# Loading the sort's keys through GpSimd's DMA queue and the small identity table through SyncE's

## The chip, the cores and the metric

The kernel runs on one core of a Trainium2 chip. The metric is the device time of one execution in microseconds (us); a smaller number is better. A core has five engines that each work through their own list of instructions in order: TensorE (PE, matrix products and transposes), VectorE (DVE), ScalarE (ACT), GpSimd (POOL) and SyncE (SP). A transfer between device memory (HBM) and on-chip memory (SBUF) is issued by one of SP, ACT and POOL; in the profile SP and ACT feed the two "hardware dynamic" queues and POOL the one "software dynamic" queue. All three queues share the core's 16 DMA engines.

## What is computed

Sixteen graphs of 1024 nodes with 64 features go through four graph layers, each followed by a residual sum and a layer norm:

```python
# layer 0: x + leaky_relu((I - sqrt(d) A / sqrt(d)) @ (batchnorm(x) @ W0 + b0)), d = row sums of A
# layer 1: attention with 8 heads, logits g0 * q.k / 8 + g1 * adj
# layer 2: per node and feature, three quantiles over the (thinned) neighbours:
vals = jnp.where(nd[..., None], x[:, None, :, :], jnp.inf)
s = jnp.sort(vals, axis=2)                 # 1024 x 1024 x 64 values per graph
agg = sum(w * interpolate(s, tau) for tau, w in ((.25, .25), (.5, .5), (.75, .25)))
#          then two dense layers with a relu
# layer 3: adj @ (x @ W3) + b3
```

The quantiles of layer 2 are by far the largest part. The kernel does not sort per node: it sorts each feature's 1024 values once per graph, ranks them, and finds the wanted rank among a node's neighbours by bit counts that TensorE sums.

## The kernel before, in words

Graphs are handled in pairs, as 128 partitions (2 graphs x 64 features) for the sort and the quantiles. The outer loop (L1193) runs p from 0 to 8 and is a software pipeline over the eight pairs. One turn p holds:

- layers 0 and 1 of pair p (`layer0` for each of the two graphs, then `attention`), for p below 8
- the sort of pair p-1 (`sort_keys`, then `sort` inside `middle`), for p from 1 on
- layers 2 and 3 of pair p-2 (`ends`, `layers23`), for p from 2 on; the last pair's come after the loop
- the quantiles of pair p-1 (`quantiles`, L782), for p from 1 on; this is the long part, about 1.05 ms of each turn

So the same passage comes up again and again: a turn's quantiles end, and the next turn starts with `sort_keys`, layer 0 of a new pair and the last layers of an old one. It comes up for p = 2 to 7 in full. At p = 1 attention, not quantiles, stands ahead of it. At p = 8 there is no layer 0.

What the passage does around the change, by name and line:

- `sort_keys` (L1155) allocates the tile `key` (128x1024 float32, 512 KB) and loads it from the scratch tensor `x2T_d` in HBM. `x2T_d` was written by POOL at the end of the pair's attention (L645).
- The eight row blocks of graph 0's adjacency matrix go to the tiles `adj0` to `adj7` (L424, SP, 512 KB each), and ACT sums their rows (L425).
- `place_tables` (L309) loads `place` (128x1024 bf16, 256 KB) and `identb` (a 128x128 bf16 identity, 32 KB); DVE makes `negidb` and `noteye` from `identb` (L315, L317).
- `layer0` (L402) loads `x0` in two halves (L407, SP), normalises it on DVE (L410, L411), transposes it on PE (L289), multiplies by the weights (L305), scales by the degrees (L415, L427, L428), and then multiplies by the transposed adjacency matrix (L392), whose row blocks `at` come through SP (L330) into four buffers. From the same `at` blocks DVE makes the neighbour masks `nbt` (L333, L334).
- `sort` (L1096) is a bitonic network of 55 steps on DVE. A step is three operations (L1105): `mask` compares, two more write the new `key`. Each mask is stored to HBM through SP (L1131) and the mask tile has four buffers.
- `layers23` (L1017) loads `x2b`, `oT`, `tof`, `agg2` (1.5 MB through ACT, L1026) and its own `at` blocks (L1056, SP).
- The quantiles end with DVE's L919 (`res`), the product of a PSUM accumulator with weights, and its store to `agg_d` by POOL (L920). There are twelve such stores per turn.

Instructions are placed on each engine's list at build time by a scheduler with a cost model, so an edit of one line can move neighbours on other engines. Two kinds of waits are then added. The first is for data and for memory: `key`, for instance, takes the place in SBUF of tiles that the quantiles still use. The second belongs to the transfers themselves: the hardware queues share eight semaphores in turn, so that a transfer waits for the landing of the one that had its semaphore before. An SP instruction that waits holds up everything that stands behind it on SP's list.

Of the kernel before, what the change touches and what calls it, by code (L numbers as in the profile page):

```python
# [25 lines left out]
P = 128  # L26
# [84 lines left out]
def gnn_kernel(ctx: ExitStack, tc: tile.TileContext, a: dict, out: bass.AP):  # L111
    nc = tc.nc
# [90 lines left out]
    x2T_d = dram.tile([B // 2 * P, N], F32, name="x2T_d")  # L203
# [105 lines left out]
    def place_tables(l0):  # L309
        place = l0.tile([P, 8 * P], BF, name="place")  # L310
        nc.sync.dma_start(place, a["c_place"])
        identb = l0.tile([P, P], BF, name="identb")
        nc.scalar.dma_start(identb, a["c_idb"])
        negidb = l0.tile([P, P], BF, name="negidb")
        nc.vector.tensor_scalar(negidb, identb, -1.0, None, op0=ALU.mult)  # L315
        noteye = l0.tile([P, P], BF, name="noteye")
        nc.vector.tensor_scalar(noteye, negidb, 1.0, None, op0=ALU.add)  # L317
        return place, identb, negidb, noteye
# [835 lines left out]

    def sort_keys(srt, ip):  # L1155
        key = srt.tile([P, N], F32, name="key", bufs=2)
        nc.sync.dma_start(key, x2T_d[ds(ip * P, P)])
        return key

    def middle(keys, srt, key, pace=()):  # L1160
# [32 lines left out]
    for p in range(B // 2 + 1):  # L1193
        with double_banks(), ExitStack() as es:
            if p >= 1:
                keys = es.enter_context(tc.tile_pool(name="keys", bufs=1, reuse_waits="tile", side="right"))
                key = sort_keys(keys, p - 1)
            last = ends(p - 2) if p >= 2 else iter(())
            if p < B // 2:
                nat = es.enter_context(tc.tile_pool(name="nat", bufs=1, reuse_waits="tile"))  # L1200
                x2 = nat.tile([P, NB, 2, C], F32, name="x2")
                graphs = [Graph(bb=bb, x1=nat.tile(NODES, F32, name=f"x1_{bb}")) for bb in range(2)]
                adj = [nat.tile([P, N], F32, name=f"adj{k}") for k in range(NB)]
                wqkv = twice(nat, "wqkv", a["WqkvT"], 3 * H * C)
                with tc.tile_pool(name="l0", bufs=1, reuse_waits="tile") as l0:
                    tables = place_tables(l0)
                    for gr in graphs:
                        gr.adj = list(adj)
                        layer0(l0, tables, p, gr.bb, None if gr.bb else adj, gr.x1)
                        if gr.bb == 0:  # L1210
                            for part in (keys_of, gates, queries_of):
                                part(gr, nat, lambda i: None)
                            for k in range(NB):
                                gated(gr, k)
                            for _ in last:
                                pass
# [43 lines left out]
```

## Time and profile before

| | |
|---|---|
| three timed runs | 13429.87, 13438.83, 13460.58 us; median 13438.83 |
| the profiled execution | 13430.77 us, of which the core's span is 13428.9 us |
| busy in the span | PE 12106.3 us (90%), DVE 10731.4 (80%), ACT 7230.1 (54%), POOL 635.6 (5%) |
| mean granted TensorE clock | 0.948 |
| moved | HBM read 380.32 MB, written 116.59 MB; 37 GB/s over the span |
| `key` loads | 8, of 512 KB, issued by SP at 623.4, 2196.5, 3838.2, 5483.5, 7132.2, 8780.7, 10425.9 and 12071.2 us |
| `identb` loads | 8, of 32 KB, issued by ACT, one per turn p = 0 to 7 |

All times below are microseconds from the start of the span. In a timeline a row gives the start, the duration, the engine (SPq and ACTq are issues of transfers), the line, the operation, what it writes and reads, and in brackets how long the engine was idle before and what ended that. In the table of stretches a row gives the stretch, its length, the busy time of PE, PE's weight loads, DVE, ACT and POOL with the number of instructions, the granted clock, the mean busy share of the 16 DMA engines and GB/s. The chain of waits is the chain of work that ended last, followed back from the end.

### The profile page before, as it was taken

The numbers are of one execution on the slowest core, as the hardware profiler recorded it, in microseconds if no ns is written. First come the engines' busy times: TensorE is split into PE (matmuls) and PEld (weight loads), VectorE is DVE, ScalarE is ACT, GpSimd is POOL, SyncE is SP. The second block draws the span as 40 slices with busy tenths as digits, with TensorE's granted clock in tenths as the row PEclk, the third lists the DMA queues.
The fourth block names the chain that finished last, engine by engine and source line by source line (L and its number), as shares of the span: only waits on it lengthen the run. The fifth ranks groups of instructions, "written<-read, shape, count | busy, mean of one in ns | idle before, by whom it ended". The sixth has DMA issues, their size and how long they took to land.

```text
span 13428.9 us, 216352 instructions
## 1 busy us (share of the span) xinstructions
PE 12106.3 (90%) x85632; PEld 5237.5 (39%) x85632; DVE 10731.4 (80%) x18699; ACT 7230.1 (54%) x13164; POOL 635.6 (5%) x948
## 2 busy tenths in 40 slices
PE   7898997989979899798997989979899799993998
PEld 4554332543325433253333633335333353331332
DVE  3587887778877788777886788877888778978895
ACT  5665554655536555365553655546455465551553
POOL 0000000000000000000000010000100001000000
PEclk9999998999989999899998999989999899996998
DMA  2110003100031000310004100041000310002001
GB/s 78 69 63 19 5 5 105 57 17 5 5 121 42 15 6 5 131 34 14 5 5 132 32 14 5 5 134 38 6 5 20 121 36 7 8 22 77 4 5 44
DMA packets 356375, 510.90 MB, mean 38 GB/s; under 512 B 124448, under 2 KB 279584, under 8 KB 353312
## 3 DMA queue, kind: packets, MB, share of 16 engines
q1 hardware_dynamic: 288656, 371.94, 8.6%
q10 hardware_dynamic: 34192, 87.14, 1.9%
q0 software_dynamic: 32512, 38.00, 1.1%
q8 instruction: 673, 11.03, 0.3%
q14 instruction: 342, 2.80, 0.1%
HBM read 380.32 MB, written 116.59 MB: 37 GB/s over the span
## 4 chain that ended last, share of the span: by engine, by line
PE 66%; DVE 14%; issue 8%; DMA 3%; ACT 3%; POOL 0%; SPq 0%; DVEq 0%; ACTq 0%; POOLq 0%
PE bank L838 31%; PE acc L838 8%; PE banks L509 6%; PE bank L545 6%; PE bank L531 6%; PE wps L838 3%; DVE m L870 2%; DMA at<-in_adjT 2%; DVE key L1105 2%; PE bank L392 1%; PE bank L488 1%; PE banks L369 1%; PE bank L847 1%; DVE lt L853 1%; DVE mask L1105 1%
## 5 line engine op out<-in xcount | busy, mean ns | idle before, releaser
L870 DVE TENSOR_TENSOR m<-V,oh 128x3072 bf16<-128x3072 bf16 x1536 | 2640.2, 1753 | 312.9 <-PE wps L838 289.3
L838 PE MATMUL bank<-ndT,E 128*128 128x512 fp8e4 x11904 | 2751.7, 381 | 7.3
L900 ACT ACTIVATE vals<-bank 128x512 f32<-128x512 f32 x3072 | 1591.8, 602 | 1399.0 <-PE bank L838 1397.0
L516 DVE CUSTOM_DVE_ANT_0 s<-banks,adj 128x1024 f32<-128x1024 f32 x1024 | 1214.5, 1222 | 801.4 <-PE banks L509 798.4
L848 ACT ACTIVATE V<-bank 128x512 uint16<-128x512 f32 x1536 | 911.8, 597 | 1742.1 <-PE bank L838 1642.4
L838 PEld LDWEIGHTS <-E 128*128 128x128 bf16 x11904 | 1117.9, 98 | 1788.6 <-issue 551.0
L862 ACT CAST oh<-bank 128x512 f16<-128x512 f32 x3072 | 1577.6, 601 | 297.5 <-PE bank L838 297.3
L838 PE MATMUL bank<-oh,bd 128*128 128x512 f16 x6144 | 1480.0, 384 | 0.0
L535 ACT COPY pT<-bank 128x512 f32<-128x512 f32 x1536 | 800.6, 594 | 800.0 <-PE bank L531 799.9
L524 ACT ACTIVATE s<-s,mx 128x1024 f32<-128x1024 f32 x1024 | 1176.8, 1161 | 90.1 <-DVE mx L516 89.2
L509 PE MATMUL banks<-kT,qT 64*128 64x512 f32 x4096 | 1094.5, 625 | 65.7 <-DVE mx L516 36.1
L853 DVE TENSOR_TENSOR lt<-V,lim 128x2048 bf16<-128x2048 uint16 x768 | 935.1, 1218 | 221.5 <-PE bank L838 220.3
L531 PEld LDWEIGHTS bank<-ident,s 128*128 128x128 f32 x8192 | 883.9, 141 | 409.9 <-issue 285.7
L531 PE MATMUL bank<-ident,s 128*128 128x128 f32 x8192 | 1017.0, 277 | 9.3 <-ACT s L524 8.7
L545 PE MATMUL bank<-pT,v 128*64 128x256 f32 x8192 | 991.7, 385 | 0.0
L838 PEld LDWEIGHTS <-bd 128*128 128x128 f16 x6144 | 542.6, 98 | 889.4 <-issue 354.2
L838 PE MATMUL bank<-lt,dif 128*128 128x512 bf16 x3072 | 813.2, 381 | 51.9 <-DVE lt L853 30.9
L838 PE MATMUL acc<-vals,bonesf 128*32 128x512 f32 x6144 | 847.6, 603 | 0.0
L838 PE MATMUL wps<-m,tonesb 128*32 128x512 bf16 x9216 | 641.6, 382 | 78.7 <-DVE m L870 78.7
L838 PE MATMUL bank<-r,pen 32*128 32x512 f16 x6144 | 487.7, 384 | 241.0 <-DVE r L757 226.9
L545 PEld LDWEIGHTS bank<-pT,v 128*64 128x64 f32 x8192 | 544.7, 136 | 306.9 <-ACT pT L535 41.3
L838 PE MATMUL acc<-oh,base 128*32 128x512 f16 x9216 | 641.8, 384 | 0.0
(248 smaller groups left out, 13323.0 us busy)
## 6 DMA issues: line engine op xcount, KB each, us to landing
at<-in_adjT SPq DMA_DIRECT2D x256, 512.0 KB, 5.5
masks_d<-mask SPq DMA_DIRECT2D x440, 128.0 KB, 1.7
mask<-masks_d SPq DMA_DIRECT2D x440, 128.0 KB, 2.1
adj<-in_adj SPq DMA_DIRECT2D x96, 512.0 KB, 5.3
ad<-in_adj ACTq DMA_DIRECT2D x64, 512.0 KB, 6.4
agg_d<-vals POOLq DMA_DIRECT2D x96, 256.0 KB, 2.3
agg<-agg_d ACTq DMA_DIRECT2D x16, 1536.0 KB, 8.0
nd_d<-nd SPq DMA_DIRECT2D x128, 128.0 KB, 1.9
```

The costliest lines, as they stand in the source:

```text
L509: then(nc.tensor.matmul(ss[h][:, hf * 512:(hf + 1) * 512], gr.qk[hp, 0][HALF[h], k * P:(k + 1) * P], gr.qk[hp, 1][HALF[h], hf * 512:(hf + ...
L516: last = nc.vector.tensor_tensor_reduce(s, ss[h], gr.adj[k], -1.0, 3.0e38, ALU.add, ALU.min, mx)
L524: then_act(nc.scalar.activation(s, s, AF.Exp, bias=mx, scale=-1.0, accum_out=sm))
L531: then(nc.tensor.transpose(ps[:, m, :], exps[h][0][:, (4 * mh + m) * P:(4 * mh + m + 1) * P], ident))
L535: then_act(nc.scalar.copy(dst, ps))
L545: then(nc.tensor.matmul(po[HALF[h]], gr.v[:, 4 * mh + m, (2 * hp + h) * C:(2 * hp + h + 1) * C], pT[h][mh][:, m, :], start=(mh == 0 and m ...
L838: then(nc.tensor.matmul(*args, **kw))
L848: nc.scalar.activation(gr.V[g][:, w, cols], ps, AF.Copy, bias=OFF)
L853: nc.vector.tensor_tensor(u.lt, gr.V[g][:, None, 0, :].to_broadcast([P, 2, N]), gr.lim[q], ALU.is_lt)
L862: nc.scalar.copy(oh[:, kk, cols], ps)
L870: nc.vector.tensor_tensor(u.m[kk], gr.V[g].bitcast(BF), u.oh[s][:, kk, None, :].to_broadcast([P, NW, N]), ALU.mult)
L900: nc.scalar.activation(vals[t], ys[t], AF.Relu)
```

## The change

Two lines change. The load of `key` moves from SP's queue to POOL's, and the load of `identb` from ACT's queue to SP's, right behind `place`. Sizes, tiles, sources and everything else stay.

```diff
     def place_tables(l0):
         place = l0.tile([P, 8 * P], BF, name="place")
         nc.sync.dma_start(place, a["c_place"])
         identb = l0.tile([P, P], BF, name="identb")
-        nc.scalar.dma_start(identb, a["c_idb"])
+        nc.sync.dma_start(identb, a["c_idb"])
...
     def sort_keys(srt, ip):
         key = srt.tile([P, N], F32, name="key", bufs=2)
-        nc.sync.dma_start(key, x2T_d[ds(ip * P, P)])
+        nc.gpsimd.dma_start(key, x2T_d[ds(ip * P, P)])
         return key
```

In the program as built the lists change near the passages only. On POOL the key's load stands directly behind the turn's last `agg_d` store (L920), or at p = 1 behind the store of `x2T_d`. On SP, `place`, `identb`, the two halves of `x0` and the first four `at` blocks stand directly behind the eight `adj` loads, and two instead of one of `layers23`'s `at` blocks come ahead of the second four of layer 0. On DVE the first four entries of a passage are the same as before (`negidb`, `noteye`, the first `mask`, one half of the new `key`); then L410 of layer 0 comes two entries earlier (and L411 two), and some operations of the following 40 us change places (L372 ahead of L437, the second graph's L410 and L411 earlier, the first graph's L455 and L460 later). About 80 us after the end of the quantiles the lists agree again.

## Prediction

> **What bounds the kernel now.** I read the page first (busy time by engine, then the chain that ended last), then the passages where the moved loads stand, by stretches of 10 us and by the timelines of SP, DVE and POOL, and asked which wait ends last there. One warning: the chain puts 2199.41 to 2208.13 down to the `agg_d` store, but DVE's wait just there is for `x0`; I go by the timeline.
>
> ```profile
> span 13428.9 us, 216352 instructions
> PE 12106.3 (90%) x85632; PEld 5237.5 (39%) x85632; DVE 10731.4 (80%) x18699; ACT 7230.1 (54%) x13164; POOL 635.6 (5%) x948
> ...
> PE 66%; DVE 14%; issue 8%; DMA 3%; ACT 3%; POOL 0%; SPq 0%; DVEq 0%; ACTq 0%; POOLq 0%
> ```
>
> TensorE carries the chain, and DMA holds only 3% of it, some 400 us over nine passages. The change touches nothing in the quantiles or attention, so it can only move the passages. The passage of p = 2 in stretches of 10 us:
>
> ```profile
> 2160.00:2170.00 10.00, 10.00 (x75) 3.06 (x71) 0.05 (x1) 4.45 (x8) 0.54 (x1) 0.73 0.92 342
> 2170.00:2180.00 10.00, 10.00 (x88) 3.26 (x82) 0.00 (x0) 4.13 (x8) 0.00 (x0) 1.00 0.26 106
> ...
> 2200.00:2210.00 10.00, 0.53 (x3) 0.53 (x4) 5.37 (x11) 0.68 (x2) 0.00 (x0) 0.64 1.05 380
> ...
> 2220.00:2230.00 10.00, 6.63 (x49) 1.95 (x47) 3.13 (x8) 1.68 (x4) 0.00 (x0) 0.67 0.94 363
> ```
>
> The DMA engines are full while the `adj` blocks come (2160 to 2170), idle from about 2173 to 2196 under PE's last quantile products, and full again from 2198 to 2240, when PE and DVE starve. SP's timeline gives the reason:
>
> ```profile
> 2159.52 4.48 SPq L424 DMA_DIRECT2D adj<-in_adj  x8
> 2196.45 0.33 SPq L1157 DMA_DIRECT2D key<-x2T_d  x1
> 2196.88 0.38 SPq L311 DMA_DIRECT2D place<-in_c_place  x1
> ...
> 2198.33 3.42 SPq L330 DMA_DIRECT2D at<-in_adjT  x4
> ```
>
> SP stands 32 us at `key`. In the program as built that load waits for the quantiles' last product with `oh` and `bd`, whose SBUF it takes over; that product ends at 2196.42. DVE in the same place:
>
> ```profile
> 2198.42 0.69 DVE L919 TENSOR_TENSOR vals<-acc,cf 128x512 f32<-128x512 f32 x1 [38.37 <-PE acc L838]
> ...
> 2207.52 0.69 DVE L410 TENSOR_TENSOR y<-x,bn_a 128x512 f32<-128x512 f32 x1 [4.31 <-DMA x<-in_x]
> ...
> 2225.45 0.70 DVE L333 TENSOR_SCALAR nbt<-at 128x1024 bf16<-128x1024 f32 x1 [3.15 <-DMA at<-in_adjT]
> ```
>
> From L919 to 2250, DVE is idle for 17.4 us: 1.1 for `identb`, 4.3 for `x0`, 8.1 for the second four `at` blocks, the rest for PE and ACT. From 2250 to 2300 it is busy without a gap, so idle time saved before 2250 is what the turn gains. The passages of p = 3 to 7 have 15.9 to 17.0 us of the same waits.
>
> **What the Trainium skill says.** "DMA: Bandwidth & Descriptors", section "Queues, rings and completion order": each DMA engine goes round the queues that have work, a packet at a time. The trace agrees: while the 12 KB packets of `agg2` move, the 4 KB packets of `at` get through at 9 per us instead of 100. Its section "Anatomy of one DMA — SWDGE (gpsimd) path" prices one at 2.0 us plus bytes over 436 GB/s: 3.2 us for `key`, as an estimate. The trace has, as medians to landing (KB each, then us):
>
> ```profile
> agg_d<-vals POOLq DMA_DIRECT2D x96, 256.0 KB, 2.3
> agg<-agg_d ACTq DMA_DIRECT2D x16, 1536.0 KB, 8.0
> ...
> x2T_d<-t_pr POOLq DMA_DIRECT2D x8, 512.0 KB, 3.7
> ```
>
> The trace's own 3.7 us for 512 KB through POOL is used; `key` itself, through SP, has 3.6. "SBUF — State Buffer", section "SBUF: two separate sides", says that GpSimd can't write descriptors while DVE runs certain operations; DVE will be idle, waiting for `key`, just then, so I add nothing.
>
> **The change, part by part (p = 2; times from L919's start at 2198.42).**
>
> *`place`, `x0` and four `at` blocks, no longer behind `key`.* As built, `place` waits for an earlier `adj` landing and for ScalarE's last write of V, long past; `x0` and `at` for landings of `adj` blocks. These 2.5 MB (0.25 + 0.25 + 4 x 0.5) move into the idle stretch. At 342 GB/s that is 7.3 us of transfer taken out of the full stretch.
>
> *`identb` to SP.* Issued near 2165, 31 us early; the 1.1 us wait goes. One issue less on ACT (0.34 us), hidden, since ACT idles 9.9 us afterwards.
>
> *`key` to POOL.* It stands behind the last `agg_d` store:
>
> ```profile
> 2199.41 0.54 POOL L920 DMA_DIRECT2D agg_d<-vals  x1 [38.52 <-DVE vals L919]
> ```
>
> So it is issued at about +1.6 instead of -2.0. The lower bound on its landing is +1.6 + 3.7 = +5.3. But this store isn't like the others: its first packet moves 4.4 us after its issue at every turn's end, against 1.1 in the middle of a turn, and at p = 2 its last at +9.9. `agg2` (issued at -0.1, 8.0 us) occupies the engines, and it still will. With the first packet at +5.4, store and key (0.75 MB) need 2.2 us at 350 GB/s, or 4.2 at the 1.4 us per 256 KB between the two POOL rows: landing +8.1 to +9.6. I take +8.8. The upper bound is the store's whole 9.9 plus another 1.4 to 2.8: +12.
>
> Behind `key` on DVE stands everything: the first `mask`, half of `key`, then L410, `key`, L411. Starts are 0.60 apart, so L411 ends 3.2 after the landing: +12.0, against +11.0 before. One more sort operation stands ahead of L428: another 0.6 late. So PE's L392 and the second four `at` loads start 1.6 us later than before (issued at +19.4 then).
>
> *Those four `at` blocks.* Before, they landed 3.2, 6.8, 8.1 and 9.9 us after issue, among a backlog. Without it PE sets the pace: 3.2 + 4 x 1.98 us (L392 at the clock of that stretch) = 11.1 after the first issue, against 14.4. That is at most 3.3 gained; with two `ad` blocks still competing I take 2.5.
>
> *Order on DVE.* L372 now stands ahead of L437 and waits for ACT's L371 (about 1.5 us more idle); waits at L372, L274 and L455 (2.1 us) shrink in turn. I take -0.4 net.
>
> Sum per passage: 2.5 - 1.6 - 0.4 = 0.5 us gained, with bounds: key at +5.3 gives 4, key at +12 loses 2.7. Six passages: 3.
>
> *p = 1.* SP stood at `key` until 623.4 because the store of `x2T_d` took 7.4 us to land. `place`, `x0` and six `adj` blocks (3.5 MB) can now start near 609 instead of 624, where the DMA share is 0.00 to 0.01. Against it: they compete with that store, so `key` lands perhaps 1.5 us later, and DVE's first 12.57 us wait grows by as much. The `at` waits (2.78, 1.44, 0.17, 1.73) mostly go. Net 3 gained (0 to 6).
>
> *p = 8.* No layer 0; DVE waits 1.82 us for `key`, sorts 9.0 us, and then waits 4.28 us for mask stores until 12088.96. `key` is now issued near 12074.7, behind a store that begins to move at 12078.5: landing near 12082. The sort reaches that point at 12091: 2 lost (0 to 4).
>
> Total: 3 + 3 - 2 = 4 us gained. The profiled execution's 13430.8 (span 13428.9) would become 13427; against the median of the runs shown, 8 us higher, 13435. The runs spread over 31 us; 0.2%, or 27 us, is about what a measurement of this kernel can tell from no change.
>
> **Rivals.** *The bytes set the passage.* If the late `key` costs little (landing near +5.3, because `agg2` alone is less in its way than today's traffic), L411 ends 2.5 us earlier and all of the 7.3 us are gained: 44 us, plus p = 1: 13395; half of it gives 13412. For: shares of 0.94 to 1.05 from 2200 to 2240. Against: L410 stands behind `key` on DVE, and L392 at 1.98 us caps the gain.
>
> *The wait for `key` takes the place of the wait for `x0`, and is longer.* Everything of layer 0 then hangs on a transfer queued behind a POOL store and 12 KB packets. Break-even is a landing near +9.3; at +12 a passage loses 2.7, and 4.5 if the second four `at` blocks gain nothing: 6 x 4.5 + 4 = 31 us, 13470. For: the store's 8.7 us. Against: much of the traffic around it has gone.
>
> *The change doesn't do what it says:* SP stays blocked by `place`'s own waits or `x2b`'s. As built, they are past; 13439.
>
> **How the numbers follow.** About even (the sum above, its own range 13415 to 13460): 0.57. Bytes: 0.22. Late key: 0.18. No effect: 0.03. The range from 13405 to 13466 leaves out the outer half of each rival. Faster by over 0.2%: 0.22; within: 0.60; slower: 0.18.
>
> **What would show it.** In the profile after: SP issues `place`, `x0` and four `at` blocks before 2180, with DMA busy from 2170 to 2180; DVE's wait for `x0` is gone and one for `key` of 7 to 8 us stands in its place; the waits at L333 fall from 8 us to about 5; at p = 8 the 4.28 us wait for masks is gone and one of about 8 us for `key` is there. I am wrong if `key` lands below 5 or above 11 us after L919, or if the sort's later steps, past 2250, don't keep what the start gains.

## The result, and the profile after

| | before | after |
|---|---|---|
| median of 20 runs each | 13447.56 us (13429.87 to 13460.58) | 13466.97 us (13455.00 to 13482.69) |
| the profiled execution's span | 13428.9 us | 13464.5 us |

The ratio is 1.0017, with a 95% interval of 1.0010 to 1.0023: the change costs about 20 us. The two spans differ by more than that, because the profiled execution of before was among its fastest; a second profile of it (below) has a span of 13445.1 us. Where a few microseconds matter, both profiles of before are used.

The page of the changed kernel, its busy times and its chain:

```profile
span 13464.5 us, 216276 instructions
PE 12127.0 (90%) x85551; PEld 5262.0 (39%) x85632; DVE 10728.6 (80%) x18699; ACT 7229.1 (54%) x13164; POOL 640.1 (5%) x956
...
PE 59%; issue 17%; DVE 13%; ACT 3%; DMA 3%; POOL 0%; SPq 0%; ACTq 0%; DVEq 0%; POOLq 0%
```

No engine became busier by anything that matters: PE's 20.7 us more lie within what two profiles of before differ by (12106.3 and 12144.8 us), and POOL's 4.5 are the issues of `key`. The chain's larger "issue" share is no finding either: it sits in the quantiles, which the change does not touch, and in the kernels below it is anything from 2% to 16% with no order by their times (2% in one of 13404 us and in one of 13481 us, 16% in one of 13513 us). The answer lies in the passages again. That of p = 2 stands 15.0 us later than before (L919 starts at 2213.43). Its stretches, with the same columns as those of before:

```profile
2175.00:2185.00 10.00, 10.00 (x75) 3.04 (x70) 0.04 (x1) 4.46 (x8) 0.54 (x1) 0.73 0.95 348
2185.00:2195.00 10.00, 10.00 (x88) 3.27 (x82) 0.00 (x0) 4.13 (x8) 0.00 (x0) 1.00 1.01 363
...
2215.00:2225.00 10.00, 0.00 (x0) 0.00 (x0) 2.06 (x4) 0.69 (x2) 0.55 (x1) 0.65 0.99 317
2225.00:2235.00 10.00, 8.01 (x31) 4.02 (x34) 9.96 (x22) 7.58 (x15) 0.00 (x0) 0.50 0.46 161
2235.00:2245.00 10.00, 5.85 (x55) 2.19 (x51) 4.17 (x9) 2.30 (x4) 0.00 (x0) 0.84 0.87 311
2245.00:2255.00 10.00, 8.04 (x52) 2.90 (x50) 5.90 (x20) 3.48 (x6) 0.00 (x0) 0.67 1.07 341
```

The idle stretch of before (share 0.26 from 2170 to 2180) is full now (1.01), so the loads did move. But the room that they left is not used: from 2225 to 2235 the DMA engines are busy for 0.46 of the time, and after 2235 they are full again. In the same place before the share was 0.99:

```profile
2210.00:2220.00 10.00, 9.32 (x43) 4.08 (x41) 8.96 (x20) 8.20 (x16) 0.00 (x0) 0.67 0.99 309
```

SP's timeline after:

```profile
2174.51 4.67 SPq L424 DMA_DIRECT2D adj<-in_adj  x8
2179.85 0.33 SPq L311 DMA_DIRECT2D place<-in_c_place  x1
2180.23 0.49 SPq L313 DMA_DIRECT2D identb<-in_c_idb  x1
2183.36 1.66 SPq L407 DMA_DIRECT2D x<-in_x  x2
2187.19 2.85 SPq L330 DMA_DIRECT2D at<-in_adjT  x4
...
2235.29 2.90 SPq L330 DMA_DIRECT2D at<-in_adjT  x4
```

`place`, `identb`, `x0` and the first four `at` blocks are issued 22 us or more before L919. The second four wait for their buffers, that is for L333 and L392, until 2235. DVE's waits in the same place, and POOL's two issues:

```profile
2213.43 0.69 DVE L919 TENSOR_TENSOR vals<-acc,cf 128x512 f32<-128x512 f32 x1 [38.39 <-PE acc L838]
...
2222.94 0.69 DVE L1105 TENSOR_TENSOR mask<-key 128x512 f16<-128x512 f32 x1 [8.48 <-DMA key<-x2T_d]
...
2225.36 0.68 DVE L411 TENSOR_TENSOR y<-y,bn_b 128x512 f32<-128x512 f32 x1
...
2240.04 0.69 DVE L333 TENSOR_SCALAR nbt<-at 128x1024 bf16<-128x1024 f32 x1 [2.64 <-DMA at<-in_adjT]
...
2244.02 0.69 DVE L333 TENSOR_SCALAR nbt<-at 128x1024 bf16<-128x1024 f32 x1 [3.03 <-DMA at<-in_adjT]
...
2250.27 0.17 DVE L344 COPY nbh<-bank 128x16 f32<-128x16 f32 x1 [2.10 <-PE bank L340]
```

```profile
2214.42 0.54 POOL L920 DMA_DIRECT2D agg_d<-vals  x1 [38.54 <-DVE negidb L315]
2215.01 0.55 POOL L1157 DMA_DIRECT2D key<-x2T_d  x1
```

The waits for `identb` (1.1 us) and `x0` (4.3 us) are gone, and one of 8.48 us for `key` stands in their place, as the prediction had it (7 to 8). L411 starts 11.9 us after L919 here (10.3 before), and L344, the copy of the neighbour counts that ends the wait for layer 0's `at` blocks, 36.8 us after it (34.7 before). The lines of before:

```profile
2208.73 0.68 DVE L411 TENSOR_TENSOR y<-y,bn_b 128x512 f32<-128x512 f32 x1
...
2233.09 0.17 DVE L344 COPY nbh<-bank 128x16 f32<-128x16 f32 x1 [1.87 <-PE bank L340]
```

Medians from issue to landing over the whole execution:

```profile
ad<-in_adj ACTq DMA_DIRECT2D x64, 512.0 KB, 3.8
agg_d<-vals POOLq DMA_DIRECT2D x96, 256.0 KB, 2.3
...
key<-x2T_d POOLq DMA_DIRECT2D x8, 512.0 KB, 8.1
```

`key` takes 8.1 us through POOL, where it took 3.6 through SP, and where the Trainium skill's "DMA: Bandwidth & Descriptors", section "Anatomy of one DMA — SWDGE (gpsimd) path", gives an estimate of 3.2; the measurement decides. The last passage, p = 8, has the longest wait:

```profile
12103.45 0.69 DVE L919 TENSOR_TENSOR vals<-acc,cf 128x512 f32<-128x512 f32 x1 [37.82 <-PE acc L838]
12114.68 0.69 DVE L1105 TENSOR_TENSOR mask<-key 128x512 f16<-128x512 f32 x1 [10.54 <-DMA key<-x2T_d]
```

### The profile page after: what moved, and what is told of

Same layout as the page of the kernel before. It is cut to its first block, busy times and chain, and to the rows that moved or that the text cites. A ratio compares the mean times of both kernels' runs of the same rounds, so it can differ in the third digit from the quotient of the medians.

```text
span 13464.5 us, 216276 instructions
## 1 busy us (share of the span) xinstructions
PE 12127.0 (90%) x85551; PEld 5262.0 (39%) x85632; DVE 10728.6 (80%) x18699; ACT 7229.1 (54%) x13164; POOL 640.1 (5%) x956
## 4 chain that ended last, share of the span: by engine, by line
PE 59%; issue 17%; DVE 13%; ACT 3%; DMA 3%; POOL 0%; SPq 0%; ACTq 0%; DVEq 0%; POOLq 0%
PE bank L838 26%; PE acc L838 6%; PE banks L509 6%; PE bank L531 6%; PE bank L545 6%; PE wps L838 3%; DVE m L870 2%; DMA at<-in_adjT 2%; DVE key L1105 2%; PE bank L392 1%; PE banks L369 1%; PE bank L488 1%; PE bank L847 1%; DVE lt L853 1%; DVE mask L1105 1%
## 5 line engine op out<-in xcount | busy, mean ns | idle before, releaser
L509 PE MATMUL banks<-kT,qT 64*128 64x512 f32 x4096 | 1092.9, 624 | 65.1 <-DVE mx L516 36.1
```

The lines of the kernel that those rows point to most:

```text
L509: then(nc.tensor.matmul(ss[h][:, hf * 512:(hf + 1) * 512], gr.qk[hp, 0][HALF[h], k * P:(k + 1) * P], gr.qk[hp, 1][HALF[h], hf * 512:(hf + ...
```

## Experiments

For each kernel the table gives means over the passages p = 2 to 7, read from its one trace in us after L919's start. "Attention" is its first L509, "time" the median against that of before on the same chip. In the text + and - are us after and before L919's start.

| kernel | first mask | second `at` block issued | second four issued | L344 | attention | time |
|---|---|---|---|---|---|---|
| before, two profiles | 2.2, 2.1 | 1.8, 1.7 | 19.2, 19.5 | 33.6, 33.5 | 218.6, 219.4 | |
| changed kernel | 9.7 | -23.9 | 21.6 | 36.1 | 220.2 | +19.4 |
| only `key` to POOL | 11.2 | -24.4 | 24.4 | 38.0 | 225.1 | +46.6 |
| only `identb` to SP | 1.7 | 1.6 | 21.4 | 36.5 | 223.4 | +28.2 |
| `key` to POOL at p = 2 to 7 | 9.6 | -24.1 | 21.6 | 36.1 | 221.2 | +20.5 |
| last store through ACT | 1.8 | 2.8 | 19.0 | 33.8 | 218.2 | +7.7 |
| `key` ahead of the store | 2.2 | -23.9 | 13.9 | 29.0 | 211.4 | -30.0 |
| the same, `identb` on ACT | 2.6 | -24.0 | 18.6 | 32.8 | 218.6 | +9.0 |
| `key` through ACT | 1.7 | 1.7 | 19.9 | 34.2 | 220.7 | +25.0 |

### The two edits one by one, and where the loss sits

Theory A: the loss sits at p = 1, at p = 8 and at the start. Theory B: each passage loses because `key` is late. Theory C: `identb` and the order of loads do it.

```diff
 only key:     -nc.sync.dma_start(key, ...)      +nc.gpsimd.dma_start(key, ...)
 only identb:  -nc.scalar.dma_start(identb, ...) +nc.sync.dma_start(identb, ...)
 p = 2 to 7:   both edits, but key through (nc.gpsimd if 0 < ip < B // 2 - 1 else nc.sync)
```

> Only the key's load moves to GpSimd's queue; identb stays on ScalarE's. Theory A (the loss sits in three places, p = 1, p = 8 and the start, and the passages p = 2 to 7 come out about even): DVE waits for key anyway when identb lands, so the late identb costs nothing; the loss is that of the changed kernel less the start's share of 1 to 7 us: 13 to 19 us slower than before. Theory B (every passage p = 2 to 7 loses 3 us or more because key lands late): 16 to 20 us slower, spread over all passages. Theory C (identb and the changed order of loads on SyncE do it): within 4 us of before.

> Only identb moves to SyncE's queue; key stays there, ahead of place and identb. Theories A and B: only the start can lose, because in the passages identb stands behind key on SyncE as place does and lands within a microsecond of its old time: 0 to 7 us slower, with attention of p = 0 starting 1 to 7 us later. Theory C: the whole loss of about 20 us.

> The changed kernel, but key goes through GpSimd's queue only at p = 2 to 7 and through SyncE's as before at p = 1 and p = 8. Theory A: 8 us of p = 1 and 5 us of p = 8 come back: 6 us slower than before (2 to 10). Theory B: the loss is in p = 2 to 7 and stays: 15 to 20 us slower.

Measured: `key` alone 13488.52 against 13441.95 us, ratio 1.0035 (1.0023 to 1.0048), 46.6 us slower; `identb` alone 13470.11, ratio 1.0020 (1.0013 to 1.0027), 28.2 us slower; `key` to POOL at p = 2 to 7, with `identb` on SP, 13462.47, ratio 1.0017 (1.0010 to 1.0024), 20.5 us slower. Each edit alone is worse than both together, which no theory had. Theory A falls with the third run: the loss stays when `key` goes through SP as before at p = 1 and p = 8. Theory B holds for that run, but not as a full account, since `identb` alone loses too and there `key` is early.

With `key` alone, SP's timeline at p = 2 (L919 at 2211.03) shows why:

```profile
2176.61 0.60 SPq L311 DMA_DIRECT2D place<-in_c_place  x1
2179.76 3.26 SPq L407 DMA_DIRECT2D x<-in_x  x2
2183.91 27.69 SPq L330 DMA_DIRECT2D at<-in_adjT  x4
```

The four issues of `at` spread over 27.69 us instead of 2.85. In the lists as built the third block has the semaphore that `identb` uses, and ACT issues `identb` only behind its last work for the quantiles, at 2209.15. So SP is held again, through a semaphore, and two blocks come 23 us later. With `identb` alone, SP stands at `key` as before, but the semaphores are dealt out anew, and ACT's first `ad` load, needed only much later, goes out earlier. ACT's issues, then DVE:

```profile
2206.99 0.34 ACTq L1026 DMA_DIRECT2D agg<-agg_d  x1
2210.13 0.33 ACTq L424 DMA_DIRECT2D ad<-in_adj  x1
```

```profile
2217.64 0.69 DVE L410 TENSOR_TENSOR y<-x,bn_a 128x512 f32<-128x512 f32 x1 [5.69 <-DMA x<-in_x]
```

`ad` is issued 3.1 us after L919 (12.3 before, behind ACT's L290), in the midst of the backlog, and DVE waits 5.69 us for `x0` instead of 4.31. That `ad` is the cause was read from this trace, not tried by itself; a rival is that `x0`, now behind `identb` on SP, is itself issued half a us later (at -0.6 and -0.2 instead of -1.1 and -0.6).

### A second profile of before

> The kernel before, unchanged, for a second profile of it. Its first profile has a span of 13428.9 us, near the fastest of its runs. A second one near the median, 13440 to 13447, would show which of the differences of 2 to 8 us at the start and at p = 1 are the change's and which belong to that one execution: if attention of p = 0 starts 4 us or more later than in the first profile, the start's share of the loss was not the change's.

The span is 13445.1 us, and attention of p = 0 starts at 191.9 us (188.1 in the first profile, 194.7 in the changed kernel). Over all kernels here that leave no work out it starts between 186.1 and 194.7, with no order by where `identb` is loaded. The start is not shown to lose anything.

### What makes `key` late

```diff
 last store through ACT:
-    nc.gpsimd.dma_start(agg_d[gr.bb][:, u.n, :], res)
+    (nc.scalar if u is units[-1] else nc.gpsimd).dma_start(agg_d[gr.bb][:, u.n, :], res)
 agg2 in thirds:
-    nc.scalar.dma_start(agg, agg_d[bb])
+    [nc.scalar.dma_start(agg[:, i:i + 2], agg_d[bb][:, i:i + 2]) for i in range(0, NU, 2)]
```

> The changed kernel, but each turn's last store to agg_d goes through ScalarE's queue, so that nothing stands ahead of key on GpSimd's queue. If the store ahead of it makes key late: key is issued some 2 us before the end of the quantiles, the first mask starts at most 3 us after L919 instead of 9.4 to 11.2, and each passage p = 2 to 8 gains 3 to 5 us on the changed kernel: 3 to 15 us faster than before. If it is the 12 KB packets of agg2 alone that make it late, wherever it stands: first mask still 6 us or more after L919, and within 6 us of the changed kernel.

> The changed kernel, but agg2 is loaded in three pieces of 512 KB with 4 KB packets instead of one of 1.5 MB with 12 KB packets. If the long packets are what keeps the last agg_d store from starting for 4.4 us, and key behind it: the store starts 1 to 2 us after its issue, first mask at +6 to +7 instead of +9.7, and each passage gains 2 to 3 us on the changed kernel. If it is the load on the DMA engines, whatever the size of its packets: first mask stays within 1 us of +9.7 and the time within 8 us of the changed kernel.

With the store through ACT, 13449.62 against 13441.95 us, ratio 1.0006 (0.9998 to 1.0014). The first mask starts 1.8 us after L919. By itself this does not show that the store ahead of `key` on POOL made it late, since ACT's list changed too: `agg2` stands behind the store there and is issued at +2.3 instead of -0.1, so its transfer is out of `key`'s way as well. The next section separates the two. The time is 7.7 us above that of before, with an interval that reaches down to no difference, where 3 to 15 us faster was expected. SP's timeline at p = 3 (L919 at 3854.91):

```profile
3829.84 29.11 SPq L330 DMA_DIRECT2D at<-in_adjT  x4
```

The second `at` block now has the semaphore of the store that moved to ACT, and stands until it has landed.

With `agg2` in thirds, 13512.78 against 13442.91 us, ratio 1.0052 (1.0038 to 1.0065), which neither side expected. The time can't be read as a test of the packets: the two extra transfers change ACT's list and the semaphores, and the second graph's first L333 starts at 77.7 us instead of 63.7. What can be read is the start of POOL's transfers. In the packet records of the changed kernel the first packet of the last store moves 5.0 to 5.3 us after L919 at p = 2 to 7; with 4 KB packets it is 4.8 to 5.3. So the packets' length is not it. In mid-turn, where the DMA engines are idle, a store's first packet moves 1.1 to 1.4 us after its issue; for the last but one store of a turn, among the eight `adj` loads, it is 3.1 to 4.0 us, and for the last 4.0 to 4.4 us. In the last two turns, which no `adj` loads follow, the last but one takes 1.1 us too. So the late start goes with the transfers that are already waiting at the engines; no run took those away alone.

### `key` first on POOL

The cleanest test leaves the lists of SP, ACT and DVE as in the changed kernel and swaps two transfers on POOL: the last result goes to the SBUF of the table `rk`, free by then, so that its store can stand behind `key`.

```diff
-    res = qn.tile([P, 512], F32, name="vals", bufs=5)
+    res = rk.rearrange("p g j c -> p (g j c)").bitcast(F32) if u is units[-1] else qn.tile(...)
...
-    nc.gpsimd.dma_start(agg_d[gr.bb][:, u.n, :], res)
+    late.append((agg_d[gr.bb][:, u.n, :], res)) if u is units[-1] else nc.gpsimd.dma_start(...)
...
-    key = sort_keys(keys, p - 1)
+    key = sort_keys(keys, p - 1); [nc.gpsimd.dma_start(*late.pop()) for _ in range(len(late))]
...
```

> The changed kernel, but each turn's last store to agg_d is issued on GpSimd behind key instead of ahead of it (its source moves to SBUF of the rank table, so that it may wait); the lists of SyncE, ScalarE and VectorE stay those of the changed kernel. Theory D1 (everything is held up by key alone, since place, x0 and four at blocks are there already): first mask 2 us after L919 instead of 9.7, L411 at +4.5 instead of +12.2, second four at loads issued at +14 instead of +21.6, and the neighbour counts (L344) 5 to 7 us earlier than in the changed kernel: 30 to 45 us faster than it over six passages and p = 8, so 10 to 25 us faster than before. Theory D2 (the transfers still to come set the pace, and the earlier start turns into longer waits for the second four at blocks): L344 at most 3 us earlier than in the changed kernel, 10 to 20 us faster than it, within 10 us of before.

Measured: 13412.96 against 13442.91 us, ratio 0.9978 (0.9968 to 0.9987): 30 us faster than before, some 50 us faster than the changed kernel, a little more than D1 expected. POOL's timeline at p = 2, then DVE's:

```profile
2209.08 0.55 POOL L1157 DMA_DIRECT2D key<-x2T_d  x1 [35.05 <-PE bank L838]
2211.77 0.54 POOL L1197 DMA_DIRECT2D agg_d<-rk  x1 [2.14 <-DVE negidb L315]
```

```profile
2210.78 0.69 DVE L919 TENSOR_TENSOR rk<-acc,cf 128x512 f32<-128x512 f32 x1 [37.58 <-PE acc L838]
...
2212.86 0.69 DVE L1105 TENSOR_TENSOR mask<-key 128x512 f16<-128x512 f32 x1 [1.05 <-DMA key<-x2T_d]
...
2215.27 0.69 DVE L411 TENSOR_TENSOR y<-y,bn_b 128x512 f32<-128x512 f32 x1
...
2230.85 0.69 DVE L333 TENSOR_SCALAR nbt<-at 128x1024 bf16<-128x1024 f32 x1 [3.53 <-DMA at<-in_adjT]
...
2241.71 0.17 DVE L344 COPY nbh<-bank 128x16 f32<-128x16 f32 x1 [1.95 <-PE bank L340]
```

The wait for `key` is 1.05 us instead of 8.48, and nothing grew in its place before L411. Each passage reaches attention 8.8 us earlier than in the changed kernel (table). Against before it is 7.6 us earlier (219.0 less 211.4). That is nearly the 7.3 us of the rival "the bytes set the passage", but the size agrees better than the reason: L411 ends 5.6 us earlier than before, where the rival had 2.5. The late `key` took all of the 7.6 us away, and 1 to 2 us more. At p = 1 the kernel loses some of its gain (598.0 us from the store of `x2T_d` to the next quantiles, 588.6 and 592.5 before).

What the store ahead of `key` does is to hold its issue back from -1.7 to +1.6, past the issue of `agg2` at -0.1. Being first on POOL is not enough where `agg2` goes out at the same time. At p = 8 of this kernel `key` is issued at -1.7 and `agg2` at -1.5, and `key` lands 8.7 us after its issue, with DVE waiting:

```profile
12054.94 0.69 DVE L1105 TENSOR_TENSOR mask<-key 128x512 f16<-128x512 f32 x1 [6.36 <-DMA key<-x2T_d]
```

With the store through ACT, where `agg2` goes out at +1.7 at p = 8, `key` lands after 3.6 us. Whether the store's own 256 KB cost `key` anything beyond the late issue was not tried.

Two more runs ask whether `key` must go through POOL for that, and whether `identb` matters once `key` is early.

```diff
 key through ACT: in the changed kernel   -nc.gpsimd.dma_start(key, ...)   +nc.scalar.dma_start(key, ...)
 identb on ACT:   in the last kernel      -nc.sync.dma_start(identb, ...)  +nc.scalar.dma_start(identb, ...)
```

> The changed kernel with key through ScalarE's queue. In the lists as built nothing late stands ahead of it there, but the second at block on SyncE now waits for the semaphore that key uses, so that it and the two behind it are issued only when key has landed, some 1.5 us after the end of the quantiles. Theory F1 (a shared semaphore of the hardware queues holds SyncE as the load itself did): first mask at +2, second at block not before +1.5, L333 of the fourth block at +14 to +15 as in the run with the store on ScalarE, L344 at +32 to +34: between 10 us faster and 8 us slower than before. Theory F2 (only the time of key counts): as with key first on GpSimd, 25 us or more faster than before.

> The kernel with key ahead of the last store on GpSimd, but identb through ScalarE's queue as before. ScalarE issues identb only after its last work for the quantiles, at about -1.9, and the third at block on SyncE has the same semaphore. Theory F1: the third and fourth at blocks are issued after identb's landing, near 0 instead of -23; 1 MB comes 3 us later, and L344 with it: 10 to 18 us faster than before instead of 30. Theory F2: identb and its place make no difference once key is early: 26 to 34 us faster than before.

`key` through ACT: 13467.71 against 13442.73 us, ratio 1.0018 (1.0012 to 1.0025). The semaphore does what F1 said: second block at +1.7, fourth L333 at +13.5, L344 at +34.2. The time is 17 us worse than F1's worst: the passages cost 1.7 us each in the end, and p = 1, which the expectation left out, costs about 10 (600.6 us from the store of `x2T_d` to the next quantiles, 588.6 and 592.5 before), since ACT now stands there for that store (its `key` is issued when the store has landed, 5.4 us after the store's issue).

`key` first with `identb` on ACT: 13451.75 us, ratio 1.0007 (0.9999 to 1.0015). The third block is issued at -0.2 instead of -23.1, and the whole gain is gone: 39 us for the place of a 32 KB load. The timelines of SP and ACT at p = 2 (L919 at 2204.69):

```profile
2178.32 27.03 SPq L330 DMA_DIRECT2D at<-in_adjT  x4
```

```profile
2202.81 0.33 ACTq L313 DMA_DIRECT2D identb<-in_c_idb  x1
```

F1 had put the loss at 12 to 20 us. L344 is 3.8 us later, near the 3 us that F1 said, and that is 23 us over six passages. Attention is 7.2 us later; the other 3.4 us arise after L344, where the lists of all engines have some operations in another order, and their cause was not traced.

### What holds the second four `at` blocks

From their issue to L344 it takes 14.4 and 14.0 us in the two profiles of before, 14.5 in the changed kernel and 15.2 with `key` first.

```diff
-    (nc.sync if adj else nc.scalar).dma_start(ad, adj2d[ds(row + k * P, P), :])
-    nc.scalar.activation(junk, ad, AF.Copy, accum_out=deg[:, k:k + 1])
+    w = slice(0, N if adj else P); (nc.sync if adj else nc.scalar).dma_start(ad[:, w], adj2d[ds(row + k * P, P), w])
+    nc.scalar.activation(junk[:, w], ad[:, w], *((AF.Copy,) if adj else (AF.Identity, eps)), accum_out=deg[:, k:k + 1])
```

> The changed kernel with an eighth of each ad block loaded and summed (128 of 1024 columns; graph 1's degrees are not the reference's): 3.5 MB less per turn, and of the blocks that compete with the second four at loads some 1.3 MB less. From the issue of these four to the neighbour counts (L344) it takes 14.4 us before, 14.5 us in the changed kernel and 15.2 us with key first, whenever they are issued. Theory E1 (these four wait for the bytes that are moved at the same time): 11 to 12.5 us in place of 14.5, which is the pace of PE. Theory E2 (they are held by something else: PE, or the transfers' semaphores): 14 us or more.

Measured: issued at 20.9, L344 at 32.3: 11.4 us, as E1 said. The sum of graph 1's rows also gets a small constant. The fourth block lands 9.2 us after the issue of the first, in the changed kernel 11.0 us. At p = 2 the last two waits for these blocks and L344's are

```profile
2257.76 0.69 DVE L333 TENSOR_SCALAR nbt<-at 128x1024 bf16<-128x1024 f32 x1 [0.29 <-DMA at<-in_adjT]
...
2259.96 0.69 DVE L333 TENSOR_SCALAR nbt<-at 128x1024 bf16<-128x1024 f32 x1 [1.25 <-DMA at<-in_adjT]
...
2261.83 0.17 DVE L344 COPY nbh<-bank 128x16 f32<-128x16 f32 x1 [0.92 <-PE bank L340]
```

So these four wait mainly for the bytes that move beside them. The test is not a clean one: a few operations of ACT and DVE change places too, and one of layer 3's blocks goes out behind the four instead of ahead of them. (This kernel as a whole took 13499.5 us in its one run: later steps came in another order, the second graph's included, and its time says nothing.)

### Two attempts at more

```diff
 key of p = 1 on SP:   (nc.gpsimd if ip else nc.sync).dma_start(key, ...)
 fifth buffer:         the same, with name="at", bufs=5 and name="at3", bufs=2 (before: 4 and 3)
```

> The kernel with key ahead of the last store, and key at p = 1 through SyncE as before, where GpSimd's queue gave it a first mask 5 us later after the store of x2T_d (15.9 us against 10.9 and 10.6 in the two profiles of before). If the late key at p = 1 costs what the traces show, 3 to 5 us faster than with key first everywhere: 33 to 36 us faster than before. If the wait there is covered by other work: the same as that kernel within 2 us, about 30 us faster than before.

> As the run before it, with five buffers for layer 0's at blocks instead of four and two instead of three for those of layer 3. If the second four at blocks set the pace by their bytes after the release of their buffers: one block of five needs no release, the other three take some 1.5 us less, L344 comes 1 to 2 us earlier in both graphs, 6 to 15 us faster than the run before it. If layer 3's blocks with two buffers then hold PE up as long: the same within 4 us.

With `key` of p = 1 on SP: 13403.78 against 13443.07 us, ratio 0.9971 (0.9959 to 0.9983), 39 us faster than before. Its interval overlaps that of the kernel without this edit, and p = 1 itself did not get shorter (597.3 us from the store to the quantiles, 598.0 without), so the 9 us between the two are not shown to be its gain. Both beat before and after.

With a fifth buffer: 13481.15 us, ratio 1.0029 (1.0017 to 1.0041). The first graph's L344 is 1.1 us earlier, as expected, but the second graph's stands at 189.8 us instead of 175.3: with two buffers for layer 3's blocks, these are late (at p = 2 the last lands at +168 instead of +153), and six passages of 13 us each make up the 77 us between the two kernels.

## Why the prediction was wrong

It said 13435 us, 4 us of gain, and the truth is 20 us of loss. Its second rival, a `key` whose wait replaces that for `x0` and is longer, was put at 13470 with a chance of 0.18. That is the kind of thing that came, and the total of 13467 lies near it, but partly by luck. The rival had 31 us of loss from a landing at +12, and 4.5 us per passage where its own terms (2.7 and 2.5) add up to 5.2; the landing was at +9.7 and the loss 19 us. The two totals meet because the median of 20 runs of before lies 9 us above that of the three runs from which the prediction counted.

- **The loads that move, and `identb`:** right. They are issued before -22 us, the idle stretch is full, and the two waits are gone.
- **`key`:** right in kind, low in size. I took a landing at +8.8 (from a sum whose lower end is 5.4 + 2.2 = 7.6 and not 8.1); the first mask starts at +9.7 on average. The packets of the store and `key` move at p = 2 from +5.3 to +8.4, as the step had it, but the landing is recorded 1.1 us after the last of them. L411 ends at 12.8 instead of 12.0. The second four `at` loads are issued 2.2 us later than before (21.6 against 19.2 and 19.5), where the step had 1.6. The break-even was put at +9.3, and the landing is past it.
- **The step that failed** is "Those four `at` blocks": a gain of 2.5 us, because without a backlog PE would set the pace with 11.1 us. The step counted to the end of the last L392. On that count the means are 13.5 and 13.1 us in the two profiles of before and 13.7 in the changed kernel (to L344: 14.4, 14.0 and 14.5), so the gain is 0. DVE's waits at L333, which were to fall from 8 us to about 5, are 7.0 us at p = 2. The backlog did not go away with the bytes that left it. Loads that are already early are no help to loads that can't start until a buffer is free; when these are released, two or three `ad` blocks and others of layer 3 move beside them. With `ad` cut to an eighth it is 10.6 us, so the pace of PE is about what is left without those bytes, and was wrong as a forecast with them.
- **The order on DVE:** 0.4 lost was the forecast; measured is 0.2 to 0.3 won back (the changed kernel is 2.6 us later than before at L344 and 2.3 us later about 95 us after L919).
- **The sum per passage:** 0.5 us gained was the forecast, 1.7 lost is measured (220.7 us to attention, the mean of the two kernels with these passages, against 219.0), 10 us over six passages.
- **p = 1:** 3 us gained was the forecast. The first mask comes 16.2 us after the store of `x2T_d` instead of 10.7, since the loads that moved ahead compete with that store, which lands after 11.4 us instead of 7.4 (I had 1.5 us for it, it is 5.5). The whole of p = 1 takes 595.9 us against 588.6 and 592.5; but it takes 592 to 601 in every variant that leaves no work out, also where `key` stayed on SP. That it loses is likely, how much is open.
- **p = 8:** 2 us lost was the forecast, 4 the bound. From L919 to the quantiles it takes 270.6 us, and 269.6 with only `key` on POOL, against 264.3 and 266.6 before and 264.7 and 265.9 in the two variants that kept `key` on SP: about 5 lost. I had the landing at about 8.9 us after L919 there; the first mask starts at 11.2.
- **p = 0:** not worked out at all. No cost of it is shown.

Passages 10, p = 8 about 5 and a few at p = 1 add up to about 20 us, but this split is not settled. The run with `key` through SP at p = 1 and p = 8 loses 20.5 us too, and the intervals of the two (13 to 31 us and 13 to 32 us) leave room for the difference. Counted from L919 to L919, a turn of p = 2 to 7 is 2.0 us longer than before in the changed kernel and 3.1 us in that run, 12 and 19 us over six turns. That the passages carry most of the loss is shown; how much p = 1 and p = 8 add is not.

The rival of the bytes (0.22) had a wrong premise: its condition, a `key` that is not late, wasn't met. The run that meets it, with `key` earlier still than the rival had it, gains 30 us, where the rival had 44. Its 7.3 us are 2.5 MB taken as 2.5 million bytes; in the 1024-byte KB of the lines it is 7.7.

## What to carry to other kernels

Before a load is moved to another queue, look at what stands ahead of it there at that moment, when that can start, and what the other queues will have in flight by then, not only at the load's own median on that queue. Bandwidth freed early is worth something only if what comes next can be issued into it: find the buffer or the wait that releases the next loads. And where queues share semaphores, look at which transfer waits for which after each edit, the small ones too: a 32 KB load behind a late ScalarE instruction held two 512 KB loads for 23 us.

## What the runs showed of the hardware

- In the changed kernel a transfer through POOL's queue started 1.1 to 1.4 us after its issue where the DMA engines were idle, and 3.1 to 4.4 us after it where transfers of the other queues were waiting; the last store started as late with `agg2` in 4 KB packets as in 12 KB ones.
- Queues with work shared the DMA engines roughly packet for packet, though the packets differ in size: at p = 8 of the kernel with `key` first, from +3 to +6, 49 packets of 4 KB moved on POOL's queue, 64 of 12 KB on ACT's and 64 of 256 bytes on SP's.
- Neither edit is good alone (46.6 and 28.2 us slower), both with the store moved behind `key` are 30 us faster, and without the edit of `identb` that kernel is 9.0 us slower. The effects of these edits don't add.
- One profiled execution can stand 16 us from another of the same kernel (13428.9 and 13445.1 us), with 3.8 us between them at the start of attention of p = 0; a single difference of 2 to 4 us at one place needs a second profile.
